# A macaron transformer block: a third pair of batches sorted by expert, with the gate and up matrices picked by a register

## The chip, the core and the metric

The kernel runs on one core of a Trainium2 chip, in float32. A core has a matrix engine (TensorE, PE in the profile, with its weight loads shown apart as PEld), three engines for elementwise work (VectorE or DVE, ScalarE or ACT, GpSimd or POOL), and SyncE (SP), which here issues most of the DMA transfers. Each engine takes its instructions in the order in which the program lists them; engines wait for each other through semaphores. The metric is the time of one execution on the device in microseconds (us).

## The reference

The input is 8 batches of 1024 tokens with 128 features. A feed-forward layer, attention, and the same feed-forward layer again are each applied to the layer-normed tokens and added to them.

```python
x = x + 0.5 * ffn(layernorm(x))      # layer 0
x = x + attention(layernorm(x))      # per batch: 1024x1024 causal, one head of 128, rotary q and k
x = x + 0.5 * ffn(layernorm(x))      # layer 1, same weights

def ffn(x):                          # 16 experts, 64 hidden units each, 4 per token
    scores = sigmoid(x @ gate_w.T)
    idx = top_k(scores + gate_b, 4)
    w = 2.5 * scores[idx] / sum(scores[idx])
    y = 0
    for e in range(16):              # the reference runs every expert over every token
        gate, up = split(x @ w13[e].T)
        y += comb[:, e] * ((silu(gate) * up) @ w2[e].T)   # comb is w at the chosen experts, else 0
    return y + shared_expert(x)
```

## The kernel before

**Two ways to do the experts.** Tokens are handled in groups of 512 (four tiles of 128; 16 groups in each layer). A *dense* group (class `Group`) runs all 16 experts over its tokens. Two experts make one pair of 128 hidden units, so there are 8 steps `k`, each a `gate` matmul (line 688) and an `up` matmul (694) of 128x128x512, a Silu on ACT (701), a product on DVE (705), and a multiplication by the token's weight (`weigh`, line 710, on DVE or on POOL, with weights that SP has broadcast into `cb`). Then come four `down` matmuls of 128x128x128 for each step (721).

A *sorted* group (class `SortedGroup`) runs only the four chosen experts of each token. Four such groups, two batches, form a `Chunk`, and `CHUNKS` lists which ones: in the kernel before, layer 1 of batches 0 and 1 and layer 1 of batches 2 and 3. A chunk counts tokens by expert (`products`, lines 967 and 968, and a chain of small DVE steps), and gives each of its 16 tiles x 128 tokens x 4 choices a place in a DRAM table `rows` of 80 tiles of 128 rows, in which every tile belongs to one expert (its *owner*). POOL then writes the rows to their places with 64 indirect DMAs (`scatter`, line 1061). The table is worked off by 10 objects of class `Rows`, of 8 tiles each, in two halves `h` of 4 tiles: SP loads the rows (1134), PE turns them (1153), PE multiplies by the owner's gate and up matrices (`up`, 1163), ACT and DVE make the hidden units (1170, 1174), PE multiplies by the owner's down matrix (1183), and SP stores the results (1196). At the end POOL fetches each token's four results with 64 indirect DMAs (`gather`, 879), and DVE adds them up (888).

**Where the expert's matrices come from.** In the kernel before, `load_experts` (1142 to 1148) reads the four owners of a half into SP registers with one load instruction, and SP then loads four 128x256 blocks of a table in DRAM (gate, up and down side by side) into the buffer `wt`. The block is the stationary operand of `up`, and the rows are the moving one, so hidden units lie along partitions and tokens along columns:

```python
nc.tensor.matmul(p[:, cols], buf("wt", (self.id, h))[:, j, :D], buf("hTs", (self.id, h))[:, cols], ...)
```

**The order of the work.** A planner (class `Plan`) writes out the order of every engine's instructions when the program is built. Each step has a duration (`work`), a rank, the steps it follows, and the buffers it takes and frees. At each point the planner takes the step that can begin first by its own clock and, among those on the engine, the one of lowest rank. On the chip the order is fixed, and only the waits move. Ranks: units 0, attention 1000 and up, sorted chunks 2000 and up, norms and routing of dense groups 3000 and up, dense experts 4000 and up. An indirect DMA on POOL is booked at 1.24 us, and after two of them in a row the planner puts in a pause (`pause`, line 269): five memsets of a spare buffer. POOL also does the power of every layer norm (`power`, 482 and 483) and the rotation of q and k (`sine` and `both`, 1296 and 1300).

**The timetable.** Layer 0 runs dense for all 16 groups, batch by batch, mixed with the attention of batches whose layer 0 is done. The two layer 1 chunks come as soon as their batches are through attention, and the eight dense groups of layer 1 (batches 4 to 7) fill the rest and the end.

Of the kernel before, what the change touches and what calls it, by code (L numbers as in the profile page):

```python
# [17 lines left out]
P = 128  # L18
# [9 lines left out]
class Step:  # L28


    def __init__(self, engine, work, rank, emit, take, free, table, moves, indexed=False,
                 port=False):
        self.indexed, self.port = indexed, port
        self.also = None
        self.engine, self.work, self.rank, self.emit = engine, work, rank, emit
        self.take, self.free, self.table, self.moves = take, free, table, moves
        self.pools = {}
        for pool, _, _ in take:
            self.pools[pool] = self.pools.get(pool, 0) + 1
        self.left, self.next, self.ready, self.end = 0, [], 0.0, None  # L40
        self.enters, self.heads, self.leaves = (), None, False


class Plan:
# [7 lines left out]
    IN_ROW, PAUSE = 2, 0.7  # L52
    RATE, LAND = 0.23, 1.9

    def __init__(self, begin, pause):
        self.pause = pause
        self.in_row = 0
        self.steps = []
        self.places = {}
        self.lines = {}  # L60
        self.held = {}
        self.free_at = dict.fromkeys(self.ENGINES, begin)
        self.transfers = begin
        self.port = begin
        self.table = None
# [9 lines left out]
    def add(self, engine, work, rank, emit, after=(), take=(), free=(), table=None, moves=0,  # L75
            indexed=False, port=False):
        s = Step(engine, work, rank, emit, take, free, table, moves, indexed, port)
        for a in after:
            if a.engine is None:
                s.ready = max(s.ready, a.end)  # L80
            else:
                a.next.append(s)
                s.left += 1
        self.steps.append(s)
        return s
# [58 lines left out]
    def run(self):  # L144
# [12 lines left out]
        while todo:  # L157
# [21 lines left out]
            if e == "POOL":  # L179
                if not s.indexed or t - self.free_at[e] > self.PAUSE:  # L180
                    self.in_row = 0
                elif self.in_row == self.IN_ROW:
                    self.pause()
                    work += self.PAUSE
                    self.in_row = 0
                self.in_row += s.indexed
# [26 lines left out]
def kernel(  # L213
# [30 lines left out]
    CHUNKS = ((1, (0, 1)), (1, (2, 3)))  # L244
# [20 lines left out]
    spare = sbuf([P, E], "spare")  # L265

    def pause():
        for _ in range(5):
            nc.gpsimd.memset(spare, 0.0)  # L269

    plan = Plan(2.0, pause)
# [3 lines left out]
    for name, n in {"gu": 3, "y": 1, "short": 3, "score": 2, "xs": 2}.items():  # L275
        plan.pool(name, n)
    buffers = {}
    for name, n, shape in (
        ("x", 9, [P, GT, D]),
        ("xn", 3, [P, GT, D]),  # L280
        ("xnc", CB * NG + 1, [P, GT, D]),
        ("hT", 3, [P, W]),
        ("hTs", 2, [P, W]),
        ("hTa", 1, [P, W]),
        ("lt", 2, [P, P]),
        ("sc", 3, [P, GT, E]),
        ("bi", 3, [P, GT, E + TOPK]),
        ("m8", 3, [P, GT, 8]),
        ("rp", 3, [P, GT, E + TOPK]),
        ("sel", 3, [P, GT, E]),  # L290
        ("comb", 3, [P, E, GT]),
        ("cT", 2, [P, P]),
        ("cb", 2, [P, NP // 2, W]),
        ("sg", 4, [P, W]),
        ("sh", 2, [P, W]),
        ("hid", NP + 2, [P, W]),
        ("q", 1, [P, S]),
        ("k", 1, [P, S]),
        ("v", 1, [P, NT, D]),
        ("pr", 2, [P, S]),  # L300
        ("prT", 2, [P, NT, P]),
        ("chosen", 1, [P, CT, E]),
        ("combc", 1, [P, CT, E]),
        ("at", 1, [P, CT, E]),
        ("eq", 1, [P, GT, TOPK, E]),
        ("row", 4, [P, GT, D]),
        ("wt", 4, [P, GT, 2 * D]),
        ("got", 4, [P, TOPK + 1, D]),
        ("hs", 2, [P, W]),
    ):  # L310
        plan.pool(name, n)
        buffers[name] = [sbuf(shape, f"{name}{m}") for m in range(n)]
# [98 lines left out]
    wqkv = sbuf([P, 3, D], "wqkv")  # L411
    cs = sbuf([P, 2, S], "cs")
# [63 lines left out]
    def norm_steps(key, b, g, rank, after, tag, uses):  # L476
# [20 lines left out]
        s = pool(1.25, UNITS, power, after=after, port=True)  # L497
        s = dve(0.2, rank, shift, after=[s], port=True)
        s = act(0.3, rank, lambda: scale(0), after=[s], take=[(tag, n, uses)])
        return chain(act, rank, [s], *[(0.3, lambda j=j: scale(j)) for j in range(1, GT)])  # L500
# [17 lines left out]
    class Group:  # L518
# [284 lines left out]
        def steps(self, p, last, after):  # L803
# [3 lines left out]
            s = norm_steps(*n, rank, after, "xn", 1)  # L807
# [8 lines left out]
    class SortedGroup(Group):  # L816
# [43 lines left out]
        def sort_steps(self, rank, after):  # L860
# [3 lines left out]
            normed = norm_steps(*n, rank, after, "xnc", 1 + TOPK * GT)  # L864
# [33 lines left out]
        def gather_steps(self, rank, after):  # L898
            ends = []
            for j in range(GT):  # L900
# [8 lines left out]
                for k in range(TOPK):  # L909
                    got = [  # L910
                        pool(
                            1.24, r, lambda j=j, k=k: self.gather(j, k),
                            after=before if k == 0 else [*after, first], moves=0.064, indexed=True,
# [17 lines left out]
    class Chunk:  # L931


        def __init__(self, n, layer, batches):
            self.n = n
# [7 lines left out]
            self.top = sbuf([P, CT, 8], f"top8_{n}")  # L943
            self.place = sbuf([P, CT, TOPK], f"place{n}", I32)
            self.owner = sbuf([1, P], f"owner{n}", I32)
# [24 lines left out]
        def sums_begin(self):  # L970
            self.at = buf("at", self.n, "chunk")
# [63 lines left out]
        def table_rows(self):  # L1035

            nc.vector.tensor_scalar(
                self.owner, bank_of(("op", self.n))[:1, :P], float(D), None, ALU.mult
            )
# [27 lines left out]
        def steps(self, rank, begins, clear):  # L1067
# [24 lines left out]
            for m in range(CB * NG):  # L1092
# [3 lines left out]
            o = dve(0.3, rank, self.table_rows, after=[o], free=end_short(b))  # L1096
            scattered = [
                pool(
                    1.24, rank, lambda t=t, k=k: self.scatter(t, k),
                    after=[placed[t // GT], cleared], free=[("xnc", self.groups[t // GT].id)],  # L1100
                    moves=0.064, indexed=True,
# [4 lines left out]
            for m in range(CB * NG):  # L1106
                w = [
                    chain(
                        dve, rank + 1, w,
# [8 lines left out]
            for i in range(NS // (2 * GT)):  # L1118
                ends, last_load[:] = Rows(self, i).steps(
                    rank + 2 + i * 0.01, o, scattered, last_load  # L1120
                )
                done += ends
            for m, gr in enumerate(self.groups):
                gr.ends = gr.gather_steps(rank + 3 + m * 0.1, [*done, *w])

    class Rows:


        def __init__(self, chunk, i):
            self.chunk, self.i, self.id = chunk, i, (chunk.n, i)  # L1130

# [7 lines left out]
        def load_experts(self, h):  # L1139
            q = 2 * self.i + h  # L1140
            w = buf("wt", (self.id, h))
            _, rows = nc.values_load_multi_w_load_instructions(
                self.chunk.owner[0:1, q * GT : (q + 1) * GT], engines=[mybir.EngineType.SP],
# [3 lines left out]
            for j, row in enumerate(rows):  # L1147
                nc.sync.dma_start(out=w[:, j, :], in_=w_table[bass.ds(row, D), :])
# [10 lines left out]
        def up(self, h):  # L1159
            p = bank_of(("xu", self.id, h))  # L1160
            for j in range(GT):
                cols = slice(j * P, (j + 1) * P)
                nc.tensor.matmul(  # L1163
                    p[:, cols], buf("wt", (self.id, h))[:, j, :D], buf("hTs", (self.id, h))[:, cols],
# [3 lines left out]
        def gate_act(self, h):  # L1168
            a = ("xu", self.id, h)
            nc.scalar.activation(buf("sg", a)[I:, :], bank_of(a)[:I, :], AF.Silu)  # L1170

        def units(self, h):
            a = ("xu", self.id, h)
            nc.vector.tensor_tensor(  # L1174
                buf("hs", self.id)[h * I : (h + 1) * I, :], bank_of(a)[I:, :],
                buf("sg", a)[I:, :], ALU.mult,
            )

        def down(self):
            for j in range(GT):  # L1180
                for h in range(2):
# [3 lines left out]
                        buf("wt", (self.id, h))[rows, j, D:],  # L1185
# [15 lines left out]
        def steps(self, rank, owner, scattered, in_front):  # L1201
            n = self.id
            w = [
                sp(
                    3.0, rank, lambda h=h: self.load_experts(h), after=[owner, *in_front],
                    take=[("wt", (n, h), 1)], moves=0.5,
                )
                for h in range(2)
            ]
            units = []  # L1210
            for h in range(2):
# [16 lines left out]
                    0.89, rank, lambda h=h: self.up(h), after=[s, w[h]],  # L1228
                    take=[*short(b), ("sg", b, 1), *([("hs", n, 1)] if h == 0 else [])],
                    free=[("hTs", a)],  # L1230
                )
                s = act(0.59, UNITS, lambda h=h: self.gate_act(h), after=[s], table="silu")
                units.append(
                    dve(
                        0.69, UNITS, lambda h=h: self.units(h),
                        after=[s, *units], free=[*end_short(b), ("sg", b)],
                    )
                )
            s = pe(
                0.95, rank, self.down, after=units,  # L1240
# [4 lines left out]
                free=[("hs", n), ("wt", (n, 0)), ("wt", (n, 1))],  # L1245
# [14 lines left out]
            return ends, [w[-1], load]  # L1260
# [3 lines left out]
    class Heads:  # L1264
# [50 lines left out]
        def steps(self, rank, begins, have):  # L1315

            b = self.b
            q, k, v = [None] * NG, [None] * NG, [None] * NG
            for g in range(NG):
                n = ("a", b, g)  # L1320
                r = rank + 0.2 * g
                s = norm_steps(*n, r, begins[g], "xn", 1)
                _, hT = turn_steps(n, r, [s], "xn", "hTa", 3)
# [24 lines left out]
                v[g] = act(0.59, r, lambda g=g: self.take_values(g), after=[s], free=end_short(a))  # L1348
            ends = [[] for _ in range(NG)]
# [128 lines left out]
    have = sp(0.5, READY, lambda: load_attention(1), after=[have], moves=1.0)  # L1478
    ends = {}
# [3 lines left out]
    def chunk_steps(n, rank, begins, clear):  # L1483
        layer, batches = CHUNKS[n]
        c = Chunk(n, layer, batches)
        c.steps(rank, begins, clear)
# [6 lines left out]
    for n, (layer, batches) in enumerate(CHUNKS):  # L1493
        if layer == 0:
            begins = {}
            for b in batches:
                for g in range(NG):
                    s = load_steps(b, g, READY, [given(16.0)], lambda b=b, g=g: load_x(b, g))
                    begins["f0", b, g] = [stats_steps("f0", b, g, READY + 1.5, [s])]
            chunk_steps(n, READY + 1.5, begins, 20.0)  # L1500
# [23 lines left out]
    for n, (layer, batches) in enumerate(CHUNKS):  # L1524
        if layer == 1:
            chunk_steps(n, SORT + 10 * n, ends, 60.0 + 100 * n)
# [80 lines left out]
```

## Time and profile before

| what | value |
|---|---|
| median of 6 runs | 938.23 us (936.97 to 942.83) |
| the profiled execution | 938.4 us, span 936.6 us |
| PE busy in the span | 904.6 us (97%) |
| DVE / ACT / POOL busy | 714.6 / 590.6 / 498.1 us |
| granted TensorE clock, mean | 0.996 |
| 64 scatters of the first / second chunk | begin at 251.4, last at 378.2 / 429.1 to 541.6 us |
| first row turned by PE, first / second chunk | 391.9 / 576.6 us |
| 64 gathers of the first / second chunk | 584.9 to 734.7 / 750.2 to 865.2 us |
| DMA moved | 136.95 MB, of it 16.79 MB by POOL's indirect DMAs |

How to read it: the span is from the first to the last instruction of the profiled execution, and the execution's own time is 1.8 us more. Busy times are unions of an engine's instructions. On the page, PE's matmuls overlap each other, so 97% says that PE nearly always has something in flight, not that it runs at its peak. A row of the groups gives a mean duration; where an engine's instructions follow each other, the distance from start to start is the price that counts.

### The profile page before, as it was taken

What the parts mean: (1) busy time and instruction counts of PE and PEld (TensorE: products, weight loads), DVE (VectorE), ACT (ScalarE), POOL (GpSimd) and SP (SyncE); (2) the same over time, 40 slices, a digit from 0 to 9 for tenths busy, and PEclk for the clock granted to TensorE, in tenths of its full rate; (3) what the DMA queues carried; (4) which work ended last, traced back from release to release, by engine and by line L of the source; (5) the groups of instructions that cost most, each with busy time, mean ns of one, the idle gap of its engine ahead of it and who ended that gap; (6) DMA issues with size and microseconds to landing.
All of it is one profiled execution on the core that took longest, in us unless ns stands there. A gap on an engine that the chain in (4) does not pass through costs nothing.

```text
span 936.6 us, 16738 instructions
## 1 busy us (share of the span) xinstructions
PE 904.6 (97%) x5226; PEld 624.9 (67%) x5226; DVE 714.6 (76%) x2161; ACT 590.6 (63%) x1058; POOL 498.1 (53%) x923
## 2 busy tenths in 40 slices
PE   8999999999999999899999999999798999999998
PEld 5575776676666667577776767767575666656665
DVE  5877868879898898598677775696769778678754
ACT  6649757989548669776656685677536856433321
POOL 3561314331488888537778740566757477677000
PEclk9999999999999999899999999999999999999999
DMA  5792627523531543547468866788667555466452
GB/s 170 166 289 58 137 65 215 129 47 92 122 99 42 126 123 81 158 114 194 149 178 245 229 183 155 204 214 224 186 189 189 128 131 123 114 148 151 113 117 51
DMA packets 147865, 136.95 MB, mean 146 GB/s; under 512 B 12160, under 2 KB 117440, under 8 KB 147648
## 3 DMA queue, kind: packets, MB, share of 16 engines
q1 hardware_dynamic: 138304, 117.83, 50.3%
q0 software_dynamic: 8192, 16.79, 6.4%
q10 hardware_dynamic: 1280, 1.26, 0.4%
q8 instruction: 41, 0.67, 0.3%
q14 instruction: 48, 0.39, 0.1%
HBM read 99.40 MB, written 36.44 MB: 145 GB/s over the span
## 4 chain that ended last, share of the span: by engine, by line
PE 72%; POOL 9%; DVE 7%; issue 4%; ACT 4%; DMA 3%; ACTq 0%; SPq 0%; DVEq 0%; POOLq 0%
PE psum L721 17%; PE psum L688 13%; PE psum L694 13%; POOL rows L1061 6%; PE psum L1418 5%; PE psum L1378 4%; PE psum L1163 4%; PE psum L1405 2%; PE psum L1183 2%; PE psum L661 2%; PE psum L1276 2%; PE psum L1153 2%; PE psum L508 2%; POOL spare L269 1%; PE psum L1305 1%
## 5 line engine op out<-in xcount | busy, mean ns | idle before, releaser
L721 PEld LDWEIGHTS psum<-wd,hid 128*128 128x128 f32 x1536 | 191.8, 192 | 50.1 <-issue 33.5
L721 PE MATMUL psum<-wd,hid 128*128 128x128 f32 x1536 | 202.6, 277 | 4.2 <-DVE hid L710 3.0
L694 PE MATMUL psum<-hT,wu 128*128 128x512 f32 x384 | 196.8, 594 | 3.9 <-DVE hid L705 3.9
L688 PE MATMUL psum<-hT,wg 128*128 128x512 f32 x384 | 198.9, 600 | 0.2 <-ACT sg L701 0.2
L701 ACT ACTIVATE sg<-psum 128x512 f32<-128x512 f32 x192 | 113.9, 597 | 121.5 <-PE psum L688 100.9
L705 DVE TENSOR_TENSOR hid<-psum,sg 128x512 f32<-128x512 f32 x192 | 131.4, 688 | 72.6 <-PE psum L694 45.4
L879 POOL DMA_INDIRECT got<-results,place x128 | 127.9, 999 | 46.7 <-issue 24.1
L1061 POOL DMA_INDIRECT rows<-xnc,place x128 | 130.6, 1021 | 36.2 <-issue 30.0
L694 PEld LDWEIGHTS psum<-hT,wu 128*128 128x128 f32 x384 | 72.9, 191 | 97.7 <-issue 85.8
L710 DVE TENSOR_TENSOR hid<-hid,cb 128x512 f32<-128x512 f32 x160 | 118.3, 745 | 4.2
L710 POOL TENSOR_TENSOR hid<-hid,cb 128x512 f32<-128x512 f32 x32 | 40.4, 1278 | 81.1 <-DVE hid L705 39.8
L1418 PEld LDWEIGHTS psum<-v,prT 128*128 128x128 f32 x576 | 70.6, 192 | 16.5 <-issue 9.5
L1418 PE MATMUL psum<-v,prT 128*128 128x128 f32 x576 | 74.1, 276 | 1.1 <-ACT prT L1409 0.9
L688 PEld LDWEIGHTS psum<-hT,wg 128*128 128x128 f32 x384 | 60.5, 192 | 18.7 <-issue 16.8
L1378 PE MATMUL psum<-k,q 128*128 128x512 f32 (+2 forms) x192 | 69.8, 489 | 1.9 <-DVE hs L1174 1.9
L1296 POOL TENSOR_TENSOR sg<-sg,cs 128x512 f32<-128x512 f32 x32 | 40.7, 1285 | 42.7 <-ACT sg L1286 42.6
L269 POOL MEMSET spare<- 128x16 f32 x450 | 51.9, 115 | 20.6
L467 DVE BATCH_NORM_STATS2 st<-x 128x6 f32<-128x128 f32 x192 | 53.2, 277 | 7.6 <-DMA x<-in_x 5.6
L1391 ACT ACTIVATE pr<-psum,top 128x128 f32<-128x128 f32 (+3 forms) x64 | 47.3, 741 | 8.6 <-DVE top L1388 3.8
L701 ACT ACT_TABLE_LOAD x40 | 51.3, 1283 | 2.3 <-PE psum L1418 1.4
L1409 ACT COPY prT<-psum 128x512 f32<-128x512 f32 (+3 forms) x82 | 37.0, 482 | 24.1 <-PE psum L1405 21.0
L888 DVE SCALAR_TENSOR_TENSOR got<-got,wk 128x128 f32<-128x128 f32 x128 | 45.9, 372 | 6.6 <-DMA got<-results,place 4.8
(146 smaller groups left out, 1476.2 us busy)
## 6 DMA issues: line engine op xcount, KB each, us to landing
cb<-cd SPq DMA_DIRECT2D x96, 512.0 KB
wt<-in_w_table SPq DMA_DIRECT2D x160, 128.0 KB
rows<-sums SPq DMA_DIRECT2D x20, 512.0 KB
row<-rows SPq DMA_DIRECT2D x40, 256.0 KB
results<-row SPq DMA_DIRECT2D x40, 256.0 KB
x<-in_x SPq DMA_DIRECT2D x16, 256.0 KB
kept<-x SPq DMA_DIRECT2D x8, 256.0 KB
rows<-xnc,place POOLq DMA_INDIRECT x128
```

What stands on the lines that cost most here:

```text
L269: nc.gpsimd.memset(spare, 0.0)
L467: nc.vector.bn_stats(st, x_of(b, t // GT)[:, t % GT, :])
L688: nc.tensor.matmul(pair_of(("gu", self.id, k))[0], wg[:, k * P : (k + 1) * P], self.hT(), start=True, stop=True,)
L694: nc.tensor.matmul(pair_of(("gu", self.id, k))[1], wu[:, k * P : (k + 1) * P], self.hT(), start=True, stop=True,)
L701: nc.scalar.activation(buf("sg", a), pair_of(a)[0], AF.Silu)
L705: nc.vector.tensor_tensor(buf("hid", a), pair_of(a)[1], buf("sg", a), ALU.mult)
L710: engine.tensor_tensor(hid, hid, cb, ALU.mult)
L721: nc.tensor.matmul(y[:, cols], units[:, cols], wsd if k == NP else wd[:, k, :], start=(self.terms[part] == 1 and j == tiles[0]), stop=(sel ...
L879: nc.gpsimd.indirect_dma_start(out=buf("got", (self.id, j))[:, k, :], out_offset=None, in_=self.chunk.results, in_offset=bass.IndirectOffs ...
L1061: nc.gpsimd.indirect_dma_start(out=self.views[t * TOPK + k], out_offset=bass.IndirectOffsetOnAxis(ap=self.place[:, t, k : k + 1], axis=0), ...
L1378: nc.tensor.matmul(s[:, c:e], q[:, i * P : self.width], k[:, c:e], start=True, stop=True)
L1418: nc.tensor.matmul(o, buf("prT", self.id)[:, j, :], buf("v", self.b)[:, j, :], start=(j == 0), stop=(j == i),)
```

## The change

It makes three chunks of two, and changes how a `Rows` object gets its matrices.

- `CHUNKS` gets a first entry: layer 0 of batches 6 and 7. Those four groups are sorted instead of dense. Their loads, norms and routing stand early (rank READY + 2.5, loads from 30 us by the planner's clock), their scatters and rows have rank SORT - 10, ahead of the layer 1 chunks. Their results go back to DRAM, and the attention of batches 6 and 7 reads them from there. The gathers of the layer 1 chunks get a later rank (SORT + 500).
- All gate and up matrices (16 x 128 x 128) are loaded once into an SBUF tile `table`, in two DMAs of 512 KB. `find_experts` reads the four owners of a half into four *PE* registers, and `up` takes the turned rows as the stationary operand and `table` at the register's place as the moving one. The product now has tokens along partitions and gate and up units along columns.
- Silu and product therefore work on 128 partitions x 256 columns, not 64 x 512. Their result `un` has to be turned by four PE transposes for each `Rows` (`turn_units`) and copied (`take_units`, to `hs`) before `down`, which is as before.
- `load_down` loads only the down matrices: eight DMAs for each `Rows` as before, but of 64x128 elements (32 KB) in place of 128x256 (128 KB).
- The pause on POOL is gone, and an indirect DMA is booked at 1.05 us.
- Small things: one more short-lived PSUM slot (`short` 3 to 4), the top-8 buffer is now shared between chunks, two lines (`plan.line`) that keep the attention norms of a batch in order, and fewer `wt` buffers.

```diff
-    CHUNKS = ((1, (0, 1)), (1, (2, 3)))
+    CHUNKS = ((0, (6, 7)), (1, (0, 1)), (1, (2, 3)))
...
-    for name, n in {"gu": 3, "y": 1, "short": 3, "score": 2, "xs": 2}.items():
+    for name, n in {"gu": 3, "y": 1, "short": 4, "score": 2, "xs": 2}.items():
...
-        ("wt", 4, [P, GT, 2 * D]),
+        ("wt", 2, [P, GT, D]),
+        ("un", 2, [P, W]),
...
-            if e == "POOL":
-                if not s.indexed or t - self.free_at[e] > self.PAUSE:
-                    self.in_row = 0
-                elif self.in_row == self.IN_ROW:
-                    self.pause()
-                    work += self.PAUSE
-                    self.in_row = 0
-                self.in_row += s.indexed
...
-        def load_experts(self, h):
+        def find_experts(self, h):
+
             q = 2 * self.i + h
-            w = buf("wt", (self.id, h))
-            _, rows = nc.values_load_multi_w_load_instructions(
-                self.chunk.owner[0:1, q * GT : (q + 1) * GT], engines=[mybir.EngineType.SP],
+            _, self.at[h] = nc.values_load_multi_w_load_instructions(
+                self.chunk.owner[0:1, q * GT : (q + 1) * GT], engines=[mybir.EngineType.PE],
                 min_val=0, max_val=(E - 1) * D,
...
         def up(self, h):
             p = bank_of(("xu", self.id, h))
+            self.find_experts(h)
             for j in range(GT):
                 cols = slice(j * P, (j + 1) * P)
                 nc.tensor.matmul(
-                    p[:, cols], buf("wt", (self.id, h))[:, j, :D], buf("hTs", (self.id, h))[:, cols],
+                    p[:, cols], buf("hTs", (self.id, h))[:, cols],
+                    table[:, bass.ds(self.at[h][j], D)],
                     start=True, stop=True,
                 )
...
+        def turn_units(self):
+            pt = tiles_of(bank_of(("xv", self.id)))
+            for j in range(GT):
+                nc.tensor.transpose(pt[:, j, :], tiles_of(buf("un", self.id))[:, j, :], ident)
+
+        def take_units(self, copy):
+            copy(buf("hs", self.id), bank_of(("xv", self.id)))
...
             scattered = [
                 pool(
-                    1.24, rank, lambda t=t, k=k: self.scatter(t, k),
+                    1.05, later, lambda t=t, k=k: self.scatter(t, k),
                     after=[placed[t // GT], cleared], free=[("xnc", self.groups[t // GT].id)],
-                    moves=0.064, indexed=True,
+                    moves=0.064,
                 )
...
-            chunk_steps(n, READY + 1.5, begins, 20.0)
+            chunk_steps(n, READY + 2.5, SORT - 10, begins, 60.0)
```

## Prediction

> **What bounds the kernel now.** I read the page first: who is busy, and who holds the chain that ended last.
>
> ```profile
> span 936.6 us, 16738 instructions
> PE 904.6 (97%) x5226; PEld 624.9 (67%) x5226; DVE 714.6 (76%) x2161; ACT 590.6 (63%) x1058; POOL 498.1 (53%) x923
> ...
> PE 72%; POOL 9%; DVE 7%; issue 4%; ACT 4%; DMA 3%; ACTq 0%; SPq 0%; DVEq 0%; POOLq 0%
> ```
>
> PE is the bound, so fewer matmuls are worth their full time as long as nobody keeps PE waiting. But 9% of the chain is POOL, an engine that is busy for only half the span. The busy times by stretch (PE, PEld, DVE, ACT, POOL) show where: while the first chunk is scattered, POOL works 107 of 128 us, and the rest is issue time between its DMAs.
>
> ```profile
> 251.40:379.20 127.80, 124.59 (x706) 84.74 (x703) 111.17 (x360) 92.50 (x174) 107.26 (x207) 1.00 0.43 107
> ```
>
> The chain in order of time, at the end of that stretch, shows what this does to PE:
>
> ```profile
> 378.15 0.97 POOL rows L1061
> 379.15 0.26 POOL mv_f L482
> 379.48 1.05 POOL mv_f L483
> 380.70 1.01 issue
> 381.71 0.69 DVE q L1289
> 382.45 0.47 PE psum L540
> 382.92 1.71 PE psum L721 x8
> 384.63 1.71 PE psum L661 x2
> ...
> 390.50 0.86 PE psum L694 x2
> ...
> 392.01 0.44 PE psum L1153 x4
> ```
>
> A norm's power (L482, L483) stood behind the scatters in POOL's queue, DVE waited for it, and PE stood still for 3.3 us. After that two matmuls of 512 columns took 1.71 us where they later take 0.86: the clock was down for about 5 us, which cost 2.8 us more (0.82 on L721, 0.85 on L661, as much on the L688 that follows, 0.3 on the next L694). So a PE wait of 3 us or more costs itself and then some 3 us.
>
> **Matmuls removed and added.** From the rows above and three more of the chain:
>
> ```profile
> 428.43 1.09 PE psum L1183 x16
> 433.81 1.78 PE psum L1163 x16
> 436.03 1.79 PE psum L721 x16
> ```
>
> A dense group's experts: 8 x (0.86 + 0.86) for gate and up, 8 x 0.89 for down, 0.1 for turning weights: 21.0 us. Four groups: -83.8. A `Rows` object after: eight transposes 0.88, `up` 1.78 (same shape, operands exchanged), four new transposes 0.44, `down` 1.09: 4.19; ten of them: +41.9. The other twenty: 20 x 0.44 = +8.8. Counting the third chunk: +1.2. Norm turns, routing and shared expert stay. Net **-31.9 us of PE**. Adding such pitches over the listed instruction order gives 877 before and 845 after, so the change does do what it says: the dense steps are gone from PE's list.
>
> **Other engines, total.** By the same count DVE's work goes from 724 to 727: 32 products of 0.69 and 34 weighings of 0.74 leave; 64 additions of gathered rows (0.37), a sort chain (some 15 us) and copies come. Silu and product of the sorted rows get cheaper (128 x 256 in place of 64 x 512, estimated 0.4 for 0.6 and 0.7). ACT falls by about 16. These lie under PE and I count them zero; without that cover they would cost some us, since between PE positions 60 and 250 DVE now has 182 us of work for 190 of PE (before 163). DMA bytes: `wt` falls by 20.5 - 7.7 = 12.8 MB and `cb` by 8; clearing, rows, results, scatter and gather of the new chunk bring some 25. At a mean busy share of a half I count nothing. SP issues eight `wt` DMAs for each `Rows` as before; what changes is that ten more `Rows` pass through its queue.
>
> **Register loads on PE.** There are 60, each with four address calculations between the matmuls. No PE register load is in this trace; the nearest rows are SP's, and PE's own waits at the same matmul:
>
> ```profile
> L1142 SPq TENSOR_LOAD <-owner x40: 293/308/1158, 250.6 to 712.3; - x40
> ...
> L1163 PEld LDWEIGHTS psum<-hTs,wt x320: 186/192/192, 394.1 to 731.7; 128*128 128x128 f32 x160
> ...
> L1163 PEldq EVENT_SEMAPHORE  x29: 51/51/831, 392.2 to 729.5; - x29
> ```
>
> PE's sequencer passed the semaphore for the first of these matmuls at 392.2; its weights were loaded at 394.1. It runs ahead of the array: at the 56 waits of the row steps (L1153 and L1163), 3 to 18 matmuls were still queued, worth 0.47 to 5.1 us, half of the time over 1.9 us. A load of 0.31 us hides in that. Lower end 0. Upper end: nothing hides, 0.31 + 4 x 0.09 (the distance of SP's address calculations) = 0.67, x 60 = 40 us. I take **+2**, near the hidden end, because of those leads. Queued behind the load are all later matmuls; they do not wait as long as the array still has work.
>
> The Trainium skill, "Runtime: NRT & Kernel Launch", section "Instruction fetch mechanics", speaks against the change: it puts a register load at about 200 ns for each register, fetched one by one over an uncached path from HBM. By it four owners would take 0.8 us, an estimate from that page, and 60 loads 48 us if nothing hid them. Here the owners lie in SBUF and SP's row has 0.308 us for all four, so the row decides.
>
> **POOL's queue.** This is where I expect part of the gain to go. POOL now has 384 indirect DMAs for 256. Their pitch without a pause:
>
> ```profile
> 588.24 0.95 POOL L879 DMA_INDIRECT got<-results,place  x1
> 589.50 0.95 POOL L879 DMA_INDIRECT got<-results,place  x1 [0.30 <-issue]
> 590.75 0.95 POOL L879 DMA_INDIRECT got<-results,place  x1 [0.31 <-issue]
> ```
>
> That is 1.26 us also in a row of three (scatters 1.27), while the new plan books 1.05: it is 13 to 14 us too early for every 64. With the pauses a pair took 3.23, so POOL gains on the old 256 and loses on the new 128: its work rises from about 590 to 680 us.
>
> First scatter stretch. In PE positions (pitches summed over the list), the counting matmuls stand at 114, batch 1's first projection at 122, the first turn of rows at 206. In the trace of before such positions come 14 us (at 217) to 17 us (at 190) late in real time. So the projection is at 136; behind it ACT's swap and four rotations on POOL (4 x 1.27) end at 144, and the first scatter follows. Until the 64th, POOL's list holds 64 x 1.27 + four rotations (5.1) + six powers (8.0) = 94.4 us: 238. Row load and landing, about 3 to 4 (256 KB at the page's 130 to 290 GB/s is 1 to 2, the rest is start; the load was issued 0.7 after the last scatter before): 242. PE is there at 206 + 17 = 223 and waits 19 us, plus 3 for the clock. All later matmuls stand behind that turn, and on SP the weight loads and `cb` loads stand behind the row load. Before lost about 7 us at its first chunk (the stretch shown above), so net **+15** (ends: -2 if the pitch were 1.05 and the clock held, +25 if the rotations come late).
>
> Later, between the last `down` of that chunk (position 359) and the first turn of the third (584), PE has 225 us of work and POOL 212: 64 gathers, 64 scatters and 51 us else. The gathers begin some 12 us after that `down`, behind batch 3's rotation and the store, and POOL will sometimes wait for PE's projections. Nearly even: **+5** (0 to 35). Removing the pause is in these pitches already.
>
> **Sum.** 936.6 - 31.9 + 2 + 15 + 5 = 926.7 of span; the profiled execution was 1.8 above its span and 0.2 above the median: **928 us** as a median. About 0.3% is what a measurement can tell from no change: 935.4 to 941.0 is the same.
>
> **Rivals.**
> 1. *POOL never holds PE.* For it: POOL's idle time before was mostly waiting for DVE (67 us each on the norms' two tiles), and being late uses up such waits. Against: the stretch above has no such waits, POOL was full. It gives 936.6 - 31.9 + 2 + 3 left = 910. Chance 0.22.
> 2. *The gathers pull the third chunk late.* In the first gather stretch of before (584.5 to 736.5) POOL was idle for 44 us in pieces, waiting for rotations, norms and weighings. Now such a stretch stands in front of the third chunk's scatters. If it idles as much, they end 44 - 13 later than PE's list allows, about 30 more: 958. It decides from about 12 us of idle that PE's own lateness does not absorb. Against: POOL late means its inputs are ready. Chance 0.22.
> 3. *Register loads run alone.* If a load waits until the array is empty, the price is the 0.67 above, 40 us: 966. Slower than before from 0.2 us exposed for each load. For it: no load on PE was ever seen; against: the leads. Chance 0.12.
> 4. *No difference to speak of* (DVE's crowding in layer 0 eats the rest): 932 to 941. Chance 0.08.
>
> My forecast, 918 to 935, gets 0.36. Faster by over 0.3%: rival 1, nearly all of the forecast, a little of rival 4: 0.58. Same 0.06. Slower: rivals 2 and 3 and scraps, 0.36. Range for 8 in 10: 907 (rival 1 with 3 to spare) to 958 (rival 2); the forecast's own range is 918 to 935.
>
> **What would show it.** Right: PE's row count falls by 64 each for L688 and L694 and 256 for `down`; POOL's scatters at 1.26 to 1.27 without memsets; one PE gap of 10 to 25 us before the first turn of rows, near 225 to 242; at PE's register loads several matmuls still queued. Wrong: PE gaps of 0.3 us or more at every `up` of `Rows` (rival 3); the largest gap before the third chunk's rows or before batch 5's or 6's scores (rival 2); no gap over 5 us at all (rival 1); or matmuls with a register as moving operand at a pitch other than 0.11 us.

## The result and the profile after

The changed kernel takes **1178.67 us** (median of 20 runs, 1170.15 to 1187.34) against 938.73 us of the kernel before beside it: 1.255 times as long, 95% interval 1.2526 to 1.2574. The forecast was 928, its range 907 to 958. The profiled execution has a span of 1181.5 us. These lines of its page answer to those shown of before:

```profile
span 1181.5 us, 17624 instructions
PE 940.4 (80%) x5364; PEld 663.9 (56%) x5364; DVE 700.8 (59%) x2253; ACT 576.9 (49%) x1078; POOL 568.8 (48%) x603
...
PE   8999947859769589858598679676796779868998
...
POOL 2635355833628570162364748767464332244540
PEclk9999979879869899888798889889897889988999
...
PE 60%; another core or an unknown queue 16%; DVE 7%; ACT 7%; issue 6%; POOL 2%; DMA 2%; SPq 0%; ACTq 0%; DVEq 0%; POOLq 0%
```

No engine is full any more, POOL included: DVE and ACT have slightly less work than before, POOL has more, and all of them wait. The chain has a part that the kernel before did not have, 16% put down to "another core or an unknown queue". There is no other core here. The list of waits (columns: waited for in all, times, longest) names the places; "remote" is a wait that the trace can put down to nobody:

```profile
engine line waited for: us in total, times, longest us
...
ACT prT L1434 <- remote: 67.5, 10, 16.2
...
DVE x L1451 <- remote: 48.9, 6, 21.7
...
ACT row L1205 <- remote: 35.4, 4, 11.0
...
DVE psum L1409 <- remote: 24.3, 4, 8.7
```

All such rows together make 301.7 us in 44 waits; the same list of the kernel before has none. Engines wait side by side here, so this is not PE's loss: of the time that PE stands still, 146 us lie inside such waits. All 44 are waits for one semaphore, the one that PE raises; none is for a signal of DVE, ACT or POOL. 78% of their time falls where POOL issues indirect DMAs back to back, which it does in 41% of the span. What such a wait looks like is in the timeline (start, length, and in brackets the idle time before it and its releaser; other lines left out):

```profile
147.03 9.07 SPq L937 DMA_DIRECT2D rows<-sums  x6
...
147.66 0.38 PE L1430 MATMUL psum<-ident,pr 128*128 128x128 f32 x2
...
147.68 1.19 POOL L1049 DMA_INDIRECT rows<-xnc,place  x1 [0.30 <-issue]
...
147.87 1.02 PE L1403 MATMUL psum<-k,q 128*128 128x512 f32 x2
149.17 0.96 POOL L1049 DMA_INDIRECT rows<-xnc,place  x1 [0.30 <-issue]
150.43 0.96 POOL L1049 DMA_INDIRECT rows<-xnc,place  x1 [0.30 <-issue]
151.70 0.96 POOL L1049 DMA_INDIRECT rows<-xnc,place  x1 [0.31 <-issue]
152.96 0.96 POOL L1049 DMA_INDIRECT rows<-xnc,place  x1 [0.30 <-issue]
154.00 0.27 ACT L1434 COPY prT<-psum 128x128 f32<-128x128 f32 x1 [7.08 <-remote]
...
154.31 0.80 PE L1443 MATMUL psum<-v,prT 128*128 128x128 f32 x2 [5.42 <-ACT prT L1434]
```

PE turns a tile of attention weights (L1430) and, by the modelled ends, is through with all that it was given at 148.9. ACT has only to copy that tile, and waits for nothing but PE's semaphore; it begins at 154.00. For five microseconds PE has nothing to do, and of the engines only POOL is at work, issuing one scatter after the other, 1.26 us apart. SP's queue is issuing six transfers that clear a table (L937); the last of that kind goes out at 344 us, and the waits go on to 1108 us, so these are not what they have in common. The trace's record of the semaphore has PE's update at 153.97, 0.02 us before ACT begins: the signal came late, not the reader. Whether PE's matmul itself ended late or only its signal is not told, since the ends of matmuls are modelled.

There is no single long wait but 75 PE gaps of over 0.4 us, 230 us in all, the long ones from 149 us to the end (before: 23 us in 21). After 24 of the 25 gaps of 2.8 us or more the granted clock falls to one half, for 3 to 20 us at a time and 235 us in all, so its mean falls from 0.996 to 0.901; most of the shorter gaps leave it as it is. To see what each kernel lost where, I took for every matmul the distance to the start of the next, and subtracted the median for its line and shape:

| us | sum of medians | excess, each under 1 us | excess, each over 1 us | head and behind the last matmul | span |
|---|---|---|---|---|---|
| before | 883.9 | 29.9 | 17.9 | 5.0 | 936.6 |
| after | 843.5 | 103.7 | 229.4 | 5.0 | 1181.5 |

(The first column is good to some 15 us: equal matmuls give 888 and 873 in two kernels below.) The matmuls fell by about 40 as the list says; waits and low clock rose by 285.

### The profile page after: what moved, and what is told of

Same layout as the page of the kernel before. It is cut to its first block, busy times and chain, and to the rows that moved or that the text cites. A ratio compares the mean times of both kernels' runs of the same rounds, so it can differ in the third digit from the quotient of the medians.

```text
span 1181.5 us, 17624 instructions
## 1 busy us (share of the span) xinstructions
PE 940.4 (80%) x5364; PEld 663.9 (56%) x5364; DVE 700.8 (59%) x2253; ACT 576.9 (49%) x1078; POOL 568.8 (48%) x603
## 3 DMA queue, kind: packets, MB, share of 16 engines
q10 hardware_dynamic: 1280, 1.26, 0.3%
## 4 chain that ended last, share of the span: by engine, by line
PE 60%; another core or an unknown queue 16%; DVE 7%; ACT 7%; issue 6%; POOL 2%; DMA 2%; SPq 0%; ACTq 0%; DVEq 0%; POOLq 0%
PE psum L708 12%; PE psum L675 10%; PE psum L681 10%; PE psum L1443 5%; PE psum L1165 4%; PE psum L1403 3%; PE psum L1430 2%; PE psum L1198 2%; PE psum L648 2%; PE psum L1154 2%; PE psum L1296 2%; PE psum L495 1%; DMA row<-rows 1%; PE psum L1189 1%
## 5 line engine op out<-in xcount | busy, mean ns | idle before, releaser
L866 POOL DMA_INDIRECT got<-results,place x192 | 188.5, 982 | 132.8 <-issue 49.9
L1049 POOL DMA_INDIRECT rows<-xnc,place x192 | 191.0, 995 | 61.9 <-issue 53.9
L708 PEld LDWEIGHTS psum<-wd,hid 128*128 128x128 f32 x1280 | 166.4, 200 | 45.8 <-issue 35.4
L708 PE MATMUL psum<-wd,hid 128*128 128x128 f32 x1280 | 175.3, 284 | 13.3 <-issue 12.0
L675 PE MATMUL psum<-hT,wg 128*128 128x512 f32 x320 | 173.2, 624 | 5.9 <-ACT row L1205 4.1
L681 PE MATMUL psum<-hT,wu 128*128 128x512 f32 x320 | 169.5, 612 | 0.9 <-DVE hTa L498 0.9
L697 DVE TENSOR_TENSOR hid<-hid,cb 128x512 f32<-128x512 f32 x126 | 87.6, 708 | 2.7
L1430 PE MATMUL psum<-ident,pr 128*128 128x128 f32 x288 | 50.6, 304 | 42.2 <-issue 15.0
L697 POOL TENSOR_TENSOR hid<-hid,cb 128x512 f32<-128x512 f32 x34 | 43.6, 1303 | 74.3 <-DMA cb<-cd 47.6
L1430 PEld LDWEIGHTS psum<-ident,pr 128*128 128x128 f32 x288 | 38.8, 157 | 58.8 <-issue 26.7
L1165 PE MATMUL psum<-table,hTs 128*128 x480 | 65.7, 283 | 3.4 <-issue 1.3
```

What stands on the lines that cost most here:

```text
L675: nc.tensor.matmul(pair_of(("gu", self.id, k))[0], wg[:, k * P : (k + 1) * P], self.hT(), start=True, stop=True,)
L681: nc.tensor.matmul(pair_of(("gu", self.id, k))[1], wu[:, k * P : (k + 1) * P], self.hT(), start=True, stop=True,)
L697: engine.tensor_tensor(hid, hid, cb, ALU.mult)
L708: nc.tensor.matmul(y[:, cols], units[:, cols], wsd if k == NP else wd[:, k, :], start=(self.terms[part] == 1 and j == tiles[0]), stop=(sel ...
L866: nc.gpsimd.indirect_dma_start(out=buf("got", (self.id, j))[:, k, :], out_offset=None, in_=self.chunk.results, in_offset=bass.IndirectOffs ...
L1049: nc.gpsimd.indirect_dma_start(out=self.views[t * TOPK + k], out_offset=bass.IndirectOffsetOnAxis(ap=self.place[:, t, k : k + 1], axis=0), ...
```

## The experiments

The kernel before ran at 929 to 947 us beside the experiments, from call to call, so kernels of different calls are compared by their ratio to it, and a difference given in us between two of them is that of the ratios. In the first four, theory P is the missing pause, R the register loads, and O the rest of the new order with its third chunk.

**e1: the pause alone, same order.** Five memsets after every two indirect DMAs that follow each other, written out without being booked:

```diff
+                if not s.indexed: self.in_row = 0
+                elif self.in_row == 2:
+                    self.pause(); self.in_row = 0
+                self.in_row += s.indexed
```

> The changed kernel with the five memsets put back on POOL after every two indirect DMAs in a row; the planner does not know of them, so every engine's other instructions stand in the changed kernel's order. Theory P (long runs of indirect DMAs without a pause make other engines' signals arrive late; the trace of the changed kernel has PE standing 5.4 us at 148.9 and 15.5 us at 235.5, both inside scatter runs): 910 to 950 us, and the many PE gaps of 5 to 16 us gone. Theory O (the plan books an indirect DMA at 1.05 while its pitch is 1.26, so the written order is wrong everywhere): POOL has another 64 to 70 us of work and the order is more wrong, 1190 to 1250. Theory R (register loads on PE): 1150 to 1200.

Measured 1045.77 us, ratio 1.1033 (1.1005 to 1.1061), outside all three ranges and nearest to P: some 142 us (133 by the bare times) came back by adding instructions to POOL. PE's gaps are fewer, not gone: 51 of over 0.4 us, 125 us in all. The chain shows what took the place of the unknown waits:

```profile
PE 50%; POOL 27%; issue 8%; DMA 6%; DVE 5%; ACT 3%; another core or an unknown queue 1%; SPq 1%; ACTq 0%; POOLq 0%; DVEq 0%
```

**e2: the pause planned,** with the planner's old bookings (1.24 us for an indirect DMA, 0.7 for a pause), so that the order moves too.

> The changed kernel with the pause, the booking of 1.24 and the booking of the pause as in the kernel before; the order is planned anew. Theory P: 905 to 940. Theory O: also 905 to 940, so only together with the run before does this tell O from P. Theory R: 1140 to 1190.

Measured 1029.08 (three runs within 1.5% of the fastest; a fourth, the traced one, took 1042.5), ratio 1.0862 (1.0803 to 1.0922). That is some 90 us above what P and O gave.

**e3: the kernel before without its pause** (the body of `pause` is `pass`; same order).

> The kernel before without the memsets of the pause; order and bookings as they were, no third chunk, no register loads on PE. Theory P: PE gaps appear inside its scatter and gather stretches; with two chunks for three, some two thirds of the 243 us: 1050 to 1120. Theory O: the indirect DMAs get earlier than booked, 930 to 940. Theory R: 930 to 940.

One execution: 1056.27 us, 109 above the kernel before beside it. The signature is the same, in a kernel without a third chunk or a register on PE:

```profile
ACT prT L1408 <- remote: 30.0, 3, 11.0
DVE prT L1408 <- remote: 24.4, 2, 12.7
DVE psum L1383 <- remote: 23.2, 2, 14.3
```

**e4: the change without register loads** (`table[:, j * D : (j + 1) * D]` in place of the register's address, so always the first four experts).

> The changed kernel with the register loads and address calculations taken off PE: up always multiplies by the first four experts' matrices, so which expert is used is not computed. Theory R: 920 to 960. Theories P and O: 1160 to 1185, since a load of 0.33 us, 60 times, is at most 20 us and mostly hidden.

One execution: 1197.19 us, no gain, and 12 above the range of P and O. The unknown waits, summed over their rows, go with the pause and not with the registers: after 302 us, e4 310, e3 160; e2 46, e1 16; before 0. R falls by this run, and O by e1 and e3; P's pause is the largest part, though its times in e1 and e2 were too good. But with its pause the changed kernel is still 9 to 10% slower than before, and the next runs are about that rest.

**e5: two chunks.** e2 with `CHUNKS = ((1, (0, 1)), (1, (2, 3)))`; the table in SBUF, the registers and `turn_units` stay.

> The kernel with the pause planned (e2_pause_planned, 1032 us) without the third chunk: batches 6 and 7 have a dense first layer again; table in SBUF, register operands, the turn of the units and the pause stay. Theory L (with the pause back, what is left is the third chunk's 128 indirect DMAs in POOL's queue, 128 x 1.62 = 207 us of it): 925 to 955. Theory T (the new way of the rows, operand from SBUF, registers, one more turn, costs by itself): 980 or more. Theory C (the third chunk's chain, in whatever queue, comes late): 925 to 955 as L.

Measured 993.08, ratio 1.0501 (1.0465 to 1.0537): neither of the two. The third chunk costs some 34 us even with the pause, and with two chunks something new costs another 5%.

**e6: the third chunk's rows by SP.** e2, but for `layer == 0` the 128 scatters and gathers are plain DMAs on SP's queue to and from fixed rows.

> The kernel with the pause planned, all three chunks, but the 64 scatters and 64 gathers of the third chunk are plain DMAs on SP's queue to and from fixed rows (row t*8+k tile by tile), so its rows are not the ones that the experts should get; the amount of work is the same. Theory L: POOL has two chunks as before, so the matmul sum's gain shows: 900 to 950. Theory C: 1000 or more, since the third chunk's own steps are all there. Theory T: 1000 or more.

Measured 996.55, ratio 1.0532 (1.0488 to 1.0577), just below the range of C and T and far above L's: 31 us better than e2, so POOL's share of the third chunk costs that much, but no better than e5. PE's last matmul ends at 962 us, 23 earlier than in e5 (985), so part of the saving is there; but POOL's gathers of the last chunk then take 31 us more behind it.

**e7: e2 without register loads.**

> The kernel with the pause planned, with the first four experts' matrices at fixed addresses in place of those that the registers pick; no register load is left on PE. Theories L and C: 1020 to 1045, no change from 1032. Theory T: 960 to 1000.

One execution: 1016.22, between the two ranges (e2's own runs lie at 1022.83 to 1042.5). This run decides nothing; e10 asks the same with two chunks.

**e8: pauses thrown together.** The kernel before with no memsets at every other pause and ten at the next.

> The kernel before with its pauses thrown together: no memsets at every other pause and ten at the next, so four (and not two) indirect DMAs follow each other, with the same number of memsets and the same order. Theory N (other engines' signals come late by the number of indirect DMAs that POOL issues without a break): between the kernel before and the one without any pause (938 and 1056), about 960 to 1010. Theory A (only the mean rate of the indirect DMAs counts): within 0.5% of the kernel before.

Measured 953.16, ratio 1.008 (1.0039 to 1.012), between the theories and nearer to A; unknown waits 7.7 us.

**e9: two chunks, gathers early.** One thing of e5 undone:

```diff
-gr.gather_steps((later if self.layer == 0 else SORT + 500 + 10 * n) + 3 + m * 0.1, ...)
+gr.gather_steps(rank + 3 + m * 0.1, ...)
```

> The kernel of e5_two_chunks (993 us; before 946 beside it) with one thing undone: the gathers of a chunk again rank right behind its rows (rank + 3), as in the kernel before, not behind all sorted work (SORT + 500). Theory G (the changed rank lets the gathers come late and crowd together): 940 to 960. Theory T (the rows' new way costs by itself: one more turn, longer chain, other DMAs): 980 to 1000. Theory S (the old order was a lucky one, and any new order of the same work costs a few per cent): 970 to 1000, in no fixed direction.

Measured 962.78, ratio 1.0232 (1.017 to 1.0295): 25 us of e5's 47 (30 against e10, below, which ran beside it). The time is just outside G's range, and the stretches are as G says. In e5 the gathers of both chunks follow each other from 554 to 855 us; in e9 they mix with the second chunk's scatters and with the norms' powers. The busy times of the stretch in which 64 gathers run, first e5, then e9 (PE, PEld, DVE, ACT, POOL, clock):

```profile
554.00:733.00 179.00, 151.57 (x964) 112.75 (x963) 107.18 (x308) 99.36 (x181) 99.17 (x190) 0.91 0.53 137
```

```profile
534.40:676.00 141.60, 131.09 (x681) 86.38 (x680) 108.84 (x334) 86.57 (x155) 116.03 (x240) 0.98 0.43 101
```

PE is idle for 27 us of the first and 10 of the second. Unknown waits: 15 us in e5, none in e9.

**e10: e5 without register loads.**

> The kernel of e5_two_chunks without register loads on PE: the first four experts' matrices stand at fixed addresses. Same order otherwise. Theory R (the loads stop PE): 950 to 970. Theories G, T and S: 985 to 1000.

Measured 994.72, ratio 1.0548 (1.0503 to 1.0592), as e5 within the intervals. The loads cost nothing that shows.

**e11: the kernel before in another order** (`HOP` 0.2 to 0.22 in the planner).

> The kernel before, with one number of its planner changed (HOP, the time booked for a signal between engines, 0.20 to 0.22): the same instructions with the same pauses, in a somewhat different order on every engine. Theory S: 2 to 6% slower than the kernel before. Theories G, T, R: within 1% of it.

Measured 939.19, ratio 0.9961 (0.994 to 0.9982). One other order is no worse, so there is no sign that the old one was lucky.

**e12: e5 with a pause of ten memsets,** 1.5 us booked.

> The kernel of e5_two_chunks with a pause of ten memsets in place of five after two indirect DMAs, and 1.5 us booked for it. Theory N2 (signals are still late in e5, since its unknown waits sum to 15 us and the kernel before has none): 950 to 975, with those waits near none. Theories T and S: 985 to 1010, since the gathers take some 60 x 0.85 us longer.

Measured 972.13, ratio 1.0292 (1.0248 to 1.0336); unknown waits none. This is as N2 says: with packed gathers, five memsets were not enough. The longer booking moved the order as well, which this run does not set apart.

**e13 to e16: does the rank explain the three chunks?** e13 is the changed kernel, e14 is e2, both with the gathers' rank taken back as in e9; e15 is e14 and e16 is e9 with ten memsets.

> The changed kernel without any pause, and only the rank of the gathers taken back to right behind their rows (three chunks). Theory G (the rank is a loss of its own, some 30 us): 1140 to 1155. Theory P (it costs only since it packs indirect DMAs closer, and with no pause at all they are packed anyhow): 1165 to 1190. If early gathers alone cured the late signals: below 1080.

> Three chunks, pause planned as in e2_pause_planned (1032), gathers right behind their rows. Theory G: 30 to 45 us less than e2, 985 to 1002, so the third chunk still costs 25 to 40 us against e9 (963). Theory G with the forecast's matmul sum right (a third chunk saves 32 us of PE once POOL does not hold it): 930 to 950. Theory L (POOL's load of three chunks): 1010 to 1030.

> As e14, with ten memsets in a pause and 1.5 us booked. Theory N2 (signals are still late with three chunks at five memsets): 15 to 30 us less than e14. Theory L: 20 to 60 us more, since 384 indirect DMAs then take some 0.43 us more each, 165 us of POOL's queue.

> Two chunks, gathers right behind their rows, pause of ten memsets. If the two gains of e9 (30) and e12 (21) have one cause, indirect DMAs packed too close: 955 to 968, no better than e9. If they are two causes: 940 to 950.

Measured 1223.58 (ratio 1.2898, 1.2805 to 1.2992), 1097.8 (1.1561, 1.151 to 1.1611), 1140.95 (1.2032, 1.1991 to 1.2072) and 999.15 (1.0547, 1.0494 to 1.0601). Three of the four are outside every range on record; only e15 is where theory L put it. With three chunks early gathers are a loss, not a gain: 66 us with the pause (e14 against e2), 33 without it (e13). And where few unknown waits were left, ten memsets cost 43 us (e15 against e14) and 30 (e16 against e9). Windows at the end of e2 and, in the second fence, of e14 show why:

```profile
1000.00:1050.00 50.00, 0.00 (x0) 0.00 (x0) 8.03 (x23) 0.00 (x0) 24.23 (x61) 0.57 0.14 40
```

```profile
960.00:1000.00 40.00, 15.93 (x104) 13.39 (x104) 5.88 (x13) 6.86 (x14) 8.81 (x23) 0.65 0.38 105
1000.00:1050.00 50.00, 0.00 (x0) 0.00 (x0) 10.90 (x31) 0.00 (x0) 36.59 (x92) 0.50 0.24 65
1050.00:1098.00 48.00, 0.00 (x0) 0.00 (x0) 9.49 (x27) 0.00 (x0) 29.49 (x76) 0.50 0.19 51
```

PE has done its last matmul at 984 to 985 us in both, and POOL is still fetching the last chunk's rows: 56 us behind it in e2, 115 in e14. In e14 the last chunk's 64 scatters are stretched over 499 to 861 us, with the other chunks' gathers (464 to 799) ahead of them and among them in POOL's queue. POOL's one queue carries 384 indirect DMAs, which at 3.18 us for a pair with its pause (the commonest distance in e2's trace) is 610 us before anything else that POOL has to do; in these two orders the last chunk comes too late.

| us | sum of medians | under 1 us | over 1 us | head and behind the last matmul | unknown waits |
|---|---|---|---|---|---|
| after | 843.5 | 103.7 | 229.4 | 5.0 | 301.7 |
| e2 pause planned | 834.2 | 74.3 | 74.6 | 57.7 | 46.0 |
| e14 and gathers early | 814.0 | 93.3 | 74.7 | 116.6 | 17 |
| e5 two chunks | 888.4 | 46.5 | 48.8 | 5.4 | 15.3 |
| e9 and gathers early | 872.6 | 48.4 | 29.4 | 5.4 | 0 |

**e17, e18: how much pause, and where.** The kernel before with five memsets after every four indirect DMAs (e17), and with pauses only between the gathers (e18).

> The kernel before with five memsets after every four indirect DMAs: runs of four as in e8 (953 beside 946), half the memsets of both, same order. If the length of a run decides: as e8, within 1.5% of the kernel before. If the mean rate decides: half of the way to the kernel without pause (1056), 980 to 1010.

> The kernel before with its pauses only between the gathers; the 128 scatters follow each other without any. If the scatters do the harm: 1030 to 1060. If the gathers do: 945 to 960. If both, by their time: 985 to 1015, with the late signals between 250 and 600 us only.

Measured 925.17, ratio 0.9952 (0.9932 to 0.9972), and 925.63, ratio 0.995 (0.9927 to 0.9974). With e11 these are the only versions that lie below the kernel before; half a per cent is too little to call them faster. Neither has an unknown wait. So e18 lies below all three of its ranges: nothing did harm there. And e17, which ran beside it, cannot tell whether the length of a run decides. Nor does e18 fit e3: up to the first gather both kernels issue the same instructions. This is the second chunk's scatter stretch in e3 (435.2 to 594.0), and then in e18:

```profile
435.20:594.00 158.80, 117.66 (x704) 85.46 (x703) 82.43 (x223) 71.73 (x127) 73.92 (x76) 0.87 0.51 143
```

```profile
424.50:533.50 109.00, 108.87 (x704) 79.06 (x701) 82.06 (x223) 71.71 (x127) 74.44 (x76) 1.00 0.74 208
```

The same 704 matmuls and 76 POOL instructions, 64 unpaused scatters among them, took 158.8 us with late signals and 109.0 us with none. So a missing pause does not make signals late every time. The two ran in different calls, with the kernel before at 947 and 929 us beside them; no run without any pause was made in the second condition. The traces differ in one more thing: e18's has a semaphore event for 1277 of PE's 1281 signals and e17's for 1279, while e3's has 1198 and no other trace here over 94%. Whether the recording of events takes part in the late signals was not tested.

Within e3 the length of a run does go with them. The first chunk's 64 scatters stand in runs of at most 9 with nothing between them, and its stretch has one unknown wait, of 0.9 us; the second chunk's stand in runs of up to 19, and eight such waits make 74 us. Other work differs between the two stretches as well, and in e18 the same runs of 19 did nothing. What else has to come together stays open.

## Why the prediction was wrong

**The step that failed** is in the paragraph on POOL's queue: "Removing the pause is in these pitches already." It took the five memsets for POOL's own time and counted their removal as 0.7 us saved for each pair. The runs show that PE's signals came late without them: put back into the changed kernel they give some 142 us (e1), left out of the kernel before they cost 109 (e3, one execution). In one later call unpaused scatters did no harm (e18), so the price depends on something that was not found. None of the four rivals was about this. Those that priced a loss priced a queue or a load, the dearest at 40 us.

**The term "later, +5 (0 to 35)" was too small as well.** It compared PE's and POOL's work up to the third chunk's first rows and found them nearly even, and did not follow POOL's queue to its end. With the pause in place the third chunk costs some 34 us (e2 against e5), and 56 us of e2's traced run lie behind the last matmul. That is POOL holding the end. Rival 2 had the right engine and a like size, but another place.

**The gathers' rank was not priced at all.** The list of what changes names it; the prediction has no step for it. With two chunks it is 25 to 30 us (e9 against e5 and e10); with three, going back costs 66 (e14).

**How the loss adds up.** From ratio to ratio, of some 239 us: the pause 142 (to e1), the bookings and the order that follows from them 16 (to e2), the third chunk 34 (to e5), the gathers' rank 25 (to e9), and 22 that no run takes apart. Undone in another order the parts would be others, as the rank shows. The pause alone is over half.

**What held.**
- The matmul sum, -31.9: gate and up have 64 rows fewer each and `down` 256, as forecast, and the sum of medians falls by 40 (good to 15). The sum is sound, but it needed a PE that nobody keeps waiting.
- Register loads, +2. These lines are the loads and what stands behind them:

```profile
L1131 PEldq TENSOR_LOAD <-owner x60: 325/333/949, 276.5 to 1010.5; - x60
...
L1165 PE MATMUL psum<-table,hTs x480: 272/275/582, 279.9 to 1013.7; 128*128 x160
...
L1165 PEldq FUSED_REGOPS  x240: 37/37/42, 277.1 to 1012.6; - x120
```

  Four owners take 0.333 us, issued 0.5 to 4.7 us ahead of the first matmul that uses them. PE's idle time before `up` is 3.4 us over all 60, and the pitch of these matmuls is 0.112 us (a product of 128x128x128 has two rows in the trace). By the Trainium skill, "Runtime: NRT & Kernel Launch", section "Instruction fetch mechanics", the four would take 0.8 us, an estimate from its 200 ns for each register; the row here is less than half of that. Rival 3 falls by e4 and e10.
- POOL's pitch, 1.26 to 1.27 without pause, as the timeline above shows. (For a pair with its pause the trace of before mostly has 3.16 to 3.19, not 3.23.) But the first scatter stretch lasted 128 us where 94 were worked out, since POOL's own inputs were late as well; POOL was busy for 76 of them, and PE for 85:

```profile
140.80:269.20 128.40, 84.79 (x415) 57.63 (x416) 62.70 (x222) 55.44 (x110) 75.96 (x80) 0.83 0.36 101
```

- The forecast gap of 10 to 25 us before the first turn of rows is not there. That turn comes at 278.6 us, not 242, and PE has no gap before it: PE was by then as late as POOL.
- "Other engines 0": DVE's and ACT's busy times fell by 14 each (DVE was to gain 3); no run charges them with the loss.

**What stays open.** Of e9's 2.3% over the kernel before, no part was singled out; the rows' longer chain, the other weight loads and the table's load are all in it. And why unpaused indirect DMAs delay signals in one condition and not in another (e3, e18) is not known, nor is what delays them. That PE's signal is late is read from the recorded semaphore events, which stand 1.6 to 18 us behind the modelled end of PE's last matmul that signals; what happens inside PE in that time no run shows.

## What to carry to other kernels

An instruction that does no work may still help other engines: price its removal by what it keeps apart, and try it alone before it goes out together with a larger change. When a chain's shares go to "unknown" and every engine's busy share falls at once, look for late signals, and look at what the one engine that is still running does in those gaps. Work that is moved from a full engine to another engine's only queue has to be followed to the end of that queue, since there it can land behind the last instruction of the engine that was relieved.

## What the runs showed of the hardware

- While POOL issued indirect DMAs 1.26 us apart, ACT and DVE stood in waits of up to 21.7 us for a signal of PE; in the one shown above, 5 us of it passed after the modelled end of PE's work. No signal of another engine came late in this way. There are 302 us of such waits in the changed kernel, 16 with five memsets (0.81 us) after every second DMA (e1), and none with ten in e12, where five had left 15 (e5).
- The effect isn't bound to the instructions alone: the stretch with the same 64 unpaused scatters took 158.8 us in one run (e3) and 109.0 in another (e18). In e3 it went with runs of up to 19 indirect DMAs, and hardly showed with runs of up to 9.
- A load of four PE registers from SBUF took 0.333 us in the median; PE's idle time before the matmuls that use them was 3.4 us over all 60 loads.
- Matmul rows whose moving operand is addressed by a PE register followed each other at 0.112 us, two for a float32 product of 128x128x128, and each address step took 0.037 us in PE's sequencer.
- After 24 of the 25 PE gaps of 2.8 us or more in the changed kernel, the granted clock was at one half for 3 to 20 us.
